# Two sums of the tail blocks moved from TensorE to GpSimd, and other durations in the clock that orders the work

## The chip, the cores and the metric

The kernel runs on one core of one Trainium2 chip. Its time is the device time of that core in microseconds (us). A core has five engines with a queue each: TensorE (PE, matrix products; its weight loads are shown as PEld), VectorE (DVE), ScalarE (ACT), GpSimd (POOL) and SyncE (SP, which here only issues DMA transfers). Each engine takes its queue strictly in order and waits at an instruction whose inputs are not there yet.

## The reference

Eight sequences of 512 rows and 128 features, float32, go through a stack with two kinds of block:

```python
x = x + 0.5 * moe(layernorm(x))            # 8 experts, 128 -> 512 -> 128, best 2 of 8 for each row
x = x + attention(layernorm(x))            # 16 heads of 8, causal, rotated q and k
x = x + 0.5 * moe(layernorm(x))            # the same weights again
x = x + 0.5 * fp6_linear(layernorm(x))     # rows rounded to 6-bit numbers in blocks of 32, times weight, + bias
x = x + scan_block(layernorm(x))           # gates g, v, d; h = a*h + sigmoid(g)*tanh(v); then a gated feed-forward
x = x + 0.5 * fp6_linear(layernorm(x))
```

In `scan_block`, with u its normed input, u becomes u + h, and the block gives u + W_out(silu(W_gate n) * (W_up n)) with n the RMS norm of u. Two sums matter below: 0.5 * bias in each `fp6_linear`, and the u that is added to what W_out gives.

## The kernel before, in words

A sequence is a tile `X[b]` of 128 partitions by 4 x 128 elements in SBUF; b runs from 0 to 7. X stays there all the time.

The first expert pass (stage 0) routes sequences 0 to 2, then 3 to 7; attention is stage 1; the second expert pass (stage 2) has the groups 0 to 4 and 5 to 7. After it come the *tails*: for each sequence `fp6`, `mix` (the scan block) and `fp6` again (`tail`, L1439). At most four tails are in flight (`flight`, L1447).

An expert pass works on row tiles of 256 rows that go to one expert. `moe_stream` (L676) routes a sequence: norm, scores (`lp`), two maxima, counts (`pt`), and then eight indirect DMAs on POOL that scatter its rows to a table in DRAM (`by_stretch`). `moe_tiles` (L846) then fetches, on SP, an expert's weights `wx` (578 KB) and 256 rows `xs` (L855 to L868), turns the rows (`xp`), and does the first product (`hp`, in two halves), the activation `hs` and the second product (`yp`); the sum `yo` goes back to DRAM on SP (`rows_out`, L922). The rows of a group are fetched only once all its sequences have been scattered (`sent`, L504). `moe_combine` (L960) gathers each row's two results on POOL (`y<-rows_out`) and adds them to X on DVE with their gates. The second group of stage 2 has 19 tiles, the first 27.

`fp6` (L1296): moments on DVE, a power on POOL (`rs`), the norm on ACT (`um`), the rounding on DVE (`am`, `sc`, `rs`, then five passes `q`), four transposes on PE (`tp_xd`), a copy on ACT (`uT_xd`), four products with the weight (`yp<-wd_t,uT_xd`) and the update of X on DVE (L1326). The bias comes into the same PSUM bank by a product of a row of ones with the bias (L1311). `mix` (L1332) goes on in the same way over all engines; its last step is the output product `yo` (L1425), into which u comes as a product with the identity (L1426), and the sum into X (L1437).

**What sets the order.** The kernel is written as generators (streams) that yield after a few instructions. All instructions of the tile streams go through the class `Clock` (L67): while the kernel is being built it estimates when each engine is free, and when a stream's next step is ready; `drive` (L146) lays side streams into attention, and `finish` (L164) always steps the stream that is ready first. So the durations that `took` (L82) returns decide the order in which instructions are put in the engines' queues, and nothing else: on the chip each engine waits for its inputs. Nearly all instructions are recorded by the helper in `_Logged`, so the profile gives them line L190; they are told apart by the names of their tiles.

Of the kernel before, what the change touches and what calls it, by code (L numbers as in the profile page):

```python
# [9 lines left out]
F32 = mybir.dt.float32  # L10
# [3 lines left out]
ALU = mybir.AluOpType  # L14
# [3 lines left out]
P = 128  # L18
S = 512
NT = S // P  # L20
# [5 lines left out]
NGF = 3  # L26
# [40 lines left out]
class Clock:  # L67
# [14 lines left out]
    def took(self, engine, op, out, args):  # L82
        shape = out.shape if out is not None else (1, 1)
        n = 1
        for k in shape[1:]:
            n *= k
        if engine == "tensor":
            strips = 4 if shape[0] == 32 or (len(args) > 1 and args[1].shape[0] == 32) else 1
            return 0.05 + 0.0016 * n / strips
        if engine == "vector":  # L90
            return 0.09 + 0.0011 * n
        if engine == "scalar":
            return 0.2 + 0.0008 * n
        if op == "indirect_dma_start":
            return 1.3
        if n <= 32:
            return 1.0
        return 0.2 + (0.0009 if op == "affine_select" else 0.0018) * n

    def account(self, ready, chained=True):  # L100

        end, last = ready, None
        product = ready
        for engine, op, out, args in self.log:
            took = self.took(engine, op, out, args)
            dep = end if chained and engine != last else ready
            if not chained and engine != "tensor":
                dep = product
            at = max(self.free[engine], dep) + took
            self.free[engine] = at  # L110
            if engine == "tensor":
                product = at
            end, last = (at if chained else max(end, at)) + 0.1, engine
            if op == "indirect_dma_start":
                end = at
            elif engine == "gpsimd":
                end += 0.5
        self.log.clear()
        return end
# [120 lines left out]
def kernel(  # L240
# [17 lines left out]
    nc = tc.nc  # L258
    ck = Clock(nc)
# [4 lines left out]
    cpool = ctx.enter_context(tc.tile_pool(name="const", bufs=1))  # L264
# [8 lines left out]
    X = []  # L273
# [24 lines left out]
    ident = cst[:, C_ID : C_ID + P]  # L298
# [51 lines left out]
    ):  # L350
        rest_of_consts[name] = (const_tile(f"{name}_s", ap, dtype), ap)
    rope_s, wattn_s, future_s, vec_s, wq8_s, wmix_s, wout_s = (t for t, _ in rest_of_consts.values())
    bq_s = cpool.tile([P, P], F32, tag="bq_s", name="bq_s")
    half_vec = cpool.tile([P, 2], F32, tag="half_vec", name="half_vec")

    clear_rows(1)
    for t, ap in rest_of_consts.values():
        nc.sync.dma_start(out=t, in_=ap)
    nc.sync.dma_start(out=bq_s, in_=bq.partition_broadcast(P))

    nstat, vpad = [], []
    for k in range(2):
# [3 lines left out]
    def clear_for_attention():  # L366

        for t in nstat:
            ck.gpsimd.memset(t, 0.0)
            yield  # L370


        for t in vpad:
            ck.gpsimd.memset(t, 0.0)
            yield
            ck.gpsimd.memset(by_pair(t)[:, :, :, DK : DK + 1], 1.0)
            yield
        ck.gpsimd.tensor_scalar_mul(half_vec[:, 0:1], vec_s[:, V_BG : V_BG + 1], 0.5)
        ck.gpsimd.tensor_scalar_mul(half_vec[:, 1:2], vec_s[:, V_BD : V_BD + 1], 0.5)
        yield  # L380
# [9 lines left out]
    def bank(name):  # L390
        return p_ps.tile([P, S], F32, tag="ps", name=name)
# [904 lines left out]
    def fp6(b, s):  # L1296

        name = f"{s}_{b}"
        mv = moments(X[b], name)
        rs = yield from power(mv[:, :, 1], 1e-5, name)  # L1300
        u = yield from normed_act(X[b], mv, rs, name, tag="um")

        xd = yield from quantized(
            u.rearrange("p t (g k) -> p (t g) k", k=FB), S // FB, name, rounding
        )
        yield from turning.take()
        tp = turned(xd.rearrange("p (t g) k -> p t (g k)", t=NT), f"xd_{name}")
        rounding.give()

        yp = bank(f"yp_{name}")  # L1310
        ck.tensor.matmul(  # L1311
            yp.rearrange("p (t d) -> p t d", t=NT), ones[0:1, :],
            bq_s[0:1].unsqueeze(1).to_broadcast([1, NT, P]), start=True, stop=False,
        )
        yield
        xt = wk.tile([P, S], F32, tag="uT", name=f"uT_xd_{name}")
        ck.scalar.copy(xt, tp)
        yield "product"
        for t in range(NT):
            ck.tensor.matmul(  # L1320
                yp[:, ts(t, P)], xt[:, ts(t, P)], wd_t, start=False, stop=(t == NT - 1)
            )
        turning.give()
        yield
        xb = X[b].rearrange("p t d -> p (t d)")
        ck.vector.scalar_tensor_tensor(xb, yp, 0.5, xb, ALU.mult, ALU.add)  # L1326
# [5 lines left out]
    def mix(b):  # L1332
# [81 lines left out]
        for f in range(NGF):  # L1414
# [6 lines left out]
            ck.vector.tensor_tensor(sg, sg, pu, ALU.mult)  # L1421
            sgs.append(sg)
            yield

        yo = bank(f"yo_{b}")  # L1425
        ck.tensor.matmul(yo, ident, uf, start=True, stop=False)  # L1426
        for t in range(NT):
            for f in range(NGF):
                ck.tensor.matmul(
                    yo[:, ts(t, P)], sgs[f][:, ts(t, P)], wout_s[:, f, :],  # L1430
                    start=False, stop=(t == NT - 1 and f == NGF - 1),
                )
        gating.give()
        feeding.give()
# [141 lines left out]
```

## Time and profile before

| | |
|---|---|
| time, median of 3 runs | 1116.26 us (1114.25 to 1118.13) |
| time of the profiled execution | 1195.04 us |
| its span, first to last instruction | 1193.3 us |
| mean granted TensorE clock in it | 0.920 |
| busy: PE, PEld | 995.5 us (83%), 693.5 us (58%) |
| busy: DVE, ACT, POOL | 683.6 us (57%), 494.9 us (41%), 472.8 us (40%) |
| moved by DMA | 127.34 MB, mean 107 GB/s |
| score products of attention, first and last | 264.0 us, 827.1 us |
| last store of an expert tile | 1042.1 us |
| last gather of expert results | 1098.2 us |

In a line of a profile a group of instructions is named by line, engine, operation and `out<-in`; `xN` counts them. Behind a bar stand busy time and the mean time of one in ns, and then the idle time of the engine before them with what ended it. In an engine's instructions in order of time, the first number is the start, the second the length, both in us, and a bracket gives the idle time before and what ended it ("issue" and "remote": nothing that the profile shows of this core's engines). A PE product of float32 is recorded as two instructions, and their times overlap.

### The profile page before, as it was taken

The page shows a single profiled execution, that of the slowest core. Times are in us where ns is not written, and L with a number is a line of the kernel's source. Part 1 is how long each engine was busy: PE and PEld are TensorE (multiplying, and loading weights), DVE is VectorE, ACT ScalarE, POOL GpSimd, SP SyncE. Part 2 cuts the span into 40 slices and gives each one's busy share as a digit, 9 for nine tenths or more (in the row PEclk, how much of TensorE's full clock was granted, in tenths as well). Part 3 has the DMA queues.
Part 4 walks back from the last instruction along what each step waited for, and adds up shares of the span by engine and source line. Part 5 has one row for each costly group of instructions (what it writes and reads, how often), then busy time and mean ns, then how long its engine had stood idle before and what let it go on. Part 6 is the DMA issues. An engine that isn't in the chain of part 4 may idle for free.

```text
span 1193.3 us, 20637 instructions
## 1 busy us (share of the span) xinstructions
PE 995.5 (83%) x6753; PEld 693.5 (58%) x6753; DVE 683.6 (57%) x2550; ACT 494.9 (41%) x1135; POOL 472.8 (40%) x627
## 2 busy tenths in 40 slices
PE   3351699799998998998998999999968898887795
PEld 2350598687774545555554567766957666554453
DVE  6040133355556888867676856532523775788755
ACT  1210233233354646464545444444312475544651
POOL 3647202331127658745363523214025452174210
PEclk9995799799999999989898889999979899995897
DMA  9542477487658001000000153334555550011000
GB/s 291 181 148 82 129 230 233 152 267 209 191 155 237 21 15 35 25 10 17 4 19 1 37 159 102 122 112 133 151 156 175 155 150 20 27 41 40 0 10 27
DMA packets 122363, 127.34 MB, mean 107 GB/s; under 512 B 9616, under 2 KB 103696, under 8 KB 122256
## 3 DMA queue, kind: packets, MB, share of 16 engines
q1 hardware_dynamic: 114064, 109.22, 30.4%
q0 software_dynamic: 8192, 16.79, 4.4%
q8 instruction: 54, 0.88, 0.3%
q14 instruction: 53, 0.43, 0.1%
HBM read 79.58 MB, written 46.40 MB: 106 GB/s over the span
## 4 chain that ended last, share of the span: by engine, by line
PE 57%; DVE 16%; issue 7%; another core or an unknown queue 7%; POOL 5%; ACT 4%; DMA 3%; SPq 1%; POOLq 0%; DVEq 0%; ACTq 0%
PE yp L190 13%; PE hp L190 11%; PE sa L190 9%; PE av L190 6%; PE sb L190 5%; DVE q L190 3%; POOL y L190 3%; DVE seen L190 2%; DVE x L190 2%; DVE st L190 1%; PE gt L190 1%; ACT um L190 1%; DMA y<-rows_out,at 1%; PE xp L190 1%
## 5 line engine op out<-in xcount | busy, mean ns | idle before, releaser
L190 DVE CUSTOM_DVE_ANT_0 seen<-sa,future_s 128x128 f32<-128x128 f32 (+3 forms) x512 | 225.2, 486 | 98.3 <-PE sb L190 70.5
L190 ACT ACTIVATE pm<-sb 128x512 f32<-128x512 f32 (+1 forms) x384 | 182.0, 525 | 205.0 <-PE sb L190 179.7
L190 PE MATMUL yp<-wx,hs 128*128 128x128 f32 x1472 | 207.3, 284 | 53.6 <-ACT hs L190 29.2
L190 ACT ACTIVATE hs<-hp,wx 128x256 f32<-128x256 f32 x276 | 119.8, 470 | 313.5 <-PE hp L190 188.4
L190 PEld LDWEIGHTS yp<-wx,hs 128*128 128x128 f32 x1472 | 193.1, 198 | 74.4 <-issue 34.5
L190 PE MATMUL sb<-qa,ka 32*128 32x512 f32 (+3 forms) x1024 | 222.7, 488 | 6.7 <-DVE nstat L190 4.8
L190 PE MATMUL sa<-ka,qz 32*128 32x384 f32 (+3 forms) x1024 | 211.3, 484 | 3.7 <-DVE nstat L190 2.5
L190 PE MATMUL hp<-xt,wx 128*128 128x256 f32 x736 | 204.5, 403 | 9.8 <-DVE g L190 5.3
L190 POOL TENSOR_SCALAR_AFFINE_SELECT pm<-pm 128x256 f32<-128x256 f32 x256 | 100.8, 409 | 240.3 <-ACT pm L190 229.3
L190 POOL DMA_INDIRECT y<-rows_out,at x128 | 134.9, 1054 | 137.7 <-DMA rows_out<-yo 77.9
L190 DVE TENSOR_SCALAR hs<-hp,wx 128x256 f32<-128x256 f32 x92 | 44.5, 483 | 214.6 <-ACT hs L190 196.6
L190 PEld LDWEIGHTS hp<-xt,wx 128*128 128x128 f32 x736 | 133.8, 201 | 39.7 <-issue 15.6
L190 PEld LDWEIGHTS sa<-ka,qz 32*128 32x128 f32 x1024 | 106.7, 194 | 71.8 <-issue 23.4
L190 PEld LDWEIGHTS sb<-qa,ka 32*128 32x128 f32 x1024 | 103.8, 190 | 30.5 <-DVE nstat L190 7.6
L190 POOL TENSOR_TENSOR rs<-rs,mhalf 128x4 f32<-128x4 f32 (+2 forms) x44 | 53.2, 1211 | 165.8 <-DVE rs L190 126.1
L190 PE MATMUL av<-pm,vpad 128*32 128x512 f32 (+3 forms) x1024 | 96.3, 472 | 2.8 <-POOL pm L190 2.6
L190 POOL DMA_INDIRECT by_stretch<-um,sat x64 | 64.3, 1005 | 30.6 <-DVE nt L190 13.4
L190 DVE SCALAR_TENSOR_TENSOR x<-y,g,x 128x128 f32<-128x128 f32 x128 | 47.5, 375 | 15.2 <-DMA y<-rows_out,at 11.0
L190 DVE TENSOR_TENSOR yo<-yp,wx 128x256 f32<-128x256 f32 x92 | 38.5, 418 | 29.8 <-PE yp L190 13.2
L190 POOL DMA_INDIRECT rows_in<-a,at x40 | 38.9, 971 | 28.2 <-issue 27.9
L190 PE MATMUL xp<-cst,xs 128*128 128x128 f32 x184 | 37.9, 293 | 11.5 <-DMA xs<-by_stretch 11.3
L190 ACT ACTIVATE um<-x,nb_um,rs 128x128 f32<-128x128 f32 x96 | 39.4, 484 | 17.2 <-DVE nb_um L190 11.3
(211 smaller groups left out, 1238.1 us busy)
## 6 DMA issues: line engine op xcount, KB each, us to landing
wx<-in_wexp SPq DMA_DIRECT2D x92, 578.0 KB
rows_out<-yo SPq DMA_DIRECT2D x92, 128.0 KB
by_stretch<-zero SPq DMA_DIRECT2D x8, 1280.0 KB
rows_in<-zero SPq DMA_DIRECT2D x2, 3456.0 KB
by_stretch<-zero SPq DMA_DIRECT2D x8, 768.0 KB
xs<-rows_in SPq DMA_DIRECT2D x46, 128.0 KB
xs<-by_stretch SPq DMA_DIRECT2D x46, 128.0 KB
x<-in_x SPq DMA_DIRECT2D x8, 256.0 KB
```

Source lines behind the costliest of these rows:

```text
L190: return call(*args, **kw)
```

## The change

Two sums leave TensorE. The bias, halved once on POOL (`half_bq`), is added to X on POOL, ahead of the products, and the product of ones with the bias goes; the four products with the weight now open the bank themselves. In `mix`, u is added to X on POOL before the output product, and the product with the identity goes. So 16 and 8 products leave, and 24 additions of 128x512 and one multiplication of 128x128 come to POOL.

`took` gives other durations for TensorE, VectorE and ScalarE, and `account` (L100) no longer lets a GpSimd `tensor_tensor` of over 1.1 us (which a 128x512 one is, by its estimate of 1.12) hold back the stream's next step. This applies to the new additions and to the two sums of the rotation in attention (`ta_q`, `ta_k`).

```diff
@@ took
         if engine == "tensor":
             strips = 4 if shape[0] == 32 or (len(args) > 1 and args[1].shape[0] == 32) else 1
-            return 0.05 + 0.0016 * n / strips
+            if op == "transpose":
+                return 0.15
+            return max(0.24, 0.02 + 0.00195 * n) if strips == 1 else 0.05 + 0.0016 * n / strips
         if engine == "vector":
-            return 0.09 + 0.0011 * n
+            return 0.17 + 0.001 * n
         if engine == "scalar":
-            return 0.2 + 0.0008 * n
+            return 0.28 + 0.00068 * n
@@ account
             self.free[engine] = at
+            if engine == "gpsimd" and op == "tensor_tensor" and took > 1.1:
+                continue
             if engine == "tensor":
                 product = at
@@ constants
-    bq_s = cpool.tile([P, P], F32, tag="bq_s", name="bq_s")
+    half_bq = cpool.tile([P, P], F32, tag="half_bq", name="half_bq")
...
-    nc.sync.dma_start(out=bq_s, in_=bq.partition_broadcast(P))
+    nc.sync.dma_start(out=half_bq, in_=bq.partition_broadcast(P))
@@ clear_for_attention
+        ck.gpsimd.tensor_scalar_mul(half_bq, half_bq, 0.5)
         ck.gpsimd.tensor_scalar_mul(half_vec[:, 0:1], vec_s[:, V_BG : V_BG + 1], 0.5)
@@ fp6
-        yp = bank(f"yp_{name}")
-        ck.tensor.matmul(
-            yp.rearrange("p (t d) -> p t d", t=NT), ones[0:1, :],
-            bq_s[0:1].unsqueeze(1).to_broadcast([1, NT, P]), start=True, stop=False,
+        ck.gpsimd.tensor_tensor(
+            X[b], X[b], half_bq.unsqueeze(1).to_broadcast([P, NT, P]), ALU.add
         )
         yield
         xt = wk.tile([P, S], F32, tag="uT", name=f"uT_xd_{name}")
         ck.scalar.copy(xt, tp)
         yield "product"
+        yp = bank(f"yp_{name}")
         for t in range(NT):
-            ck.tensor.matmul(
-                yp[:, ts(t, P)], xt[:, ts(t, P)], wd_t, start=False, stop=(t == NT - 1)
-            )
+            ck.tensor.matmul(yp[:, ts(t, P)], xt[:, ts(t, P)], wd_t, start=True, stop=True)
@@ mix
-
+        ck.gpsimd.tensor_tensor(X[b], X[b], u, ALU.add)
         yo = bank(f"yo_{b}")
-        ck.tensor.matmul(yo, ident, uf, start=True, stop=False)
         for t in range(NT):
             for f in range(NGF):
                 ck.tensor.matmul(
                     yo[:, ts(t, P)], sgs[f][:, ts(t, P)], wout_s[:, f, :],
-                    start=False, stop=(t == NT - 1 and f == NGF - 1),
+                    start=(f == 0), stop=(f == NGF - 1),
                 )
```

## The prediction

> **What bounds the kernel now.** First I read the page's busy times, then stretches of the span by engine, then each engine in order of time where the stretches show idle TensorE.
>
> ```profile
> PE 995.5 (83%) x6753; PEld 693.5 (58%) x6753; DVE 683.6 (57%) x2550; ACT 494.9 (41%) x1135; POOL 472.8 (40%) x627
> 867.00:892.00 25.00, 13.70 (x76) 11.41 (x75) 6.41 (x22) 2.61 (x7) 4.86 (x5) 0.76 0.46 144
> 892.00:1041.00 149.00, 131.03 (x704) 100.40 (x703) 91.91 (x286) 76.87 (x197) 59.98 (x55) 0.94 0.37 111
> 1041.00:1193.30 152.30, 115.06 (x460) 68.79 (x458) 108.19 (x306) 69.05 (x173) 47.00 (x41) 0.83 0.08 24
> ```
>
> TensorE is the bound over all (83%). The three stretches (columns: length, busy PE, weight loads, DVE, ACT, POOL, clock, DMA) are where the change works: a hole of 25 us, the last 19 expert tiles mixed with the first tails, and tails alone. In the last PE is busy 76% and DVE 71%: neither is a bound by itself; the in-order queues are.
>
> The hole, on PE, then on SP's queue, then on ACT:
>
> ```profile
> 877.24 4.16 PE L190 MATMUL yp<-wx,hs 128*128 128x128 f32 x24
> 885.49 0.66 PE L190 MATMUL xp<-cst,xs 128*128 128x128 f32 x2 [4.08 <-DMA xs<-by_stretch]
> 888.55 0.69 PE L190 MATMUL xp<-cst,xs 128*128 128x128 f32 x2 [2.40 <-DMA xs<-by_stretch]
> 891.63 0.69 PE L190 MATMUL xp<-cst,xs 128*128 128x128 f32 x2 [2.39 <-DMA xs<-by_stretch]
> ```
> ```profile
> 860.73 19.27 SPq L922 DMA_DIRECT2D rows_out<-yo  x5
> 880.87 0.35 SPq L857 DMA_DIRECT2D wx<-in_wexp  x1
> 882.63 0.39 SPq L868 DMA_DIRECT2D xs<-by_stretch  x1
> ```
> ```profile
> 871.84 0.84 ACT L190 ACTIVATE hs<-hp,wx 128x256 f32<-128x256 f32 x2 [4.75 <-issue]
> 874.68 1.20 ACT L190 ACTIVATE hs<-hp,wx 128x256 f32<-128x256 f32 x3 [2.00 <-remote]
> ```
>
> The second expert pass has 27 tiles for its first group and 19 for its second; the second group's may be fetched only after the last sequence (7) is routed and scattered. Its scatters end at 873.2, but SP stands behind five stores of the first group's last tiles until 880, because the fetches were written into its queue after them. PE has nothing left and waits for xs three times. Tiles run 3.75 us apart before this (first halves start at 859.96, 863.69, 867.43). The first half of tile 26 starts at 870.94, so the next tile was due at 874.7; it comes at 892.1: 17.4 us lost, of which ACT's two pauses (6.75 us) are not SP's doing.
>
> **The change part by part.**
>
> *The build clock* gives other durations, so the queues are written in another order though no work differs. I compared the two built orders.
>
> (a) Up to the middle of attention nearly nothing moves (first PE difference: row 422 of 2138). Routing of the second pass stands 26 to 50 score matmuls later, and the first expert tile of that pass 44 later; at the end of attention 2.8 fewer tiles are done. Those 2.8 tiles are then left as cover: before, 4.5 tiles follow the routing's count matmul (pt, 857.4); after, 7, or 26 us. SP's queue now has the fetches of the second group's first two tiles ahead of the stores of tiles 23 and 24. Counting from pt: scatters end at +15.8 (row 873.2 minus 857.4), land about +18, the first xs is fetched at +18.5 and lands at +21.5 (882.63 to 885.49 is 2.9), the second some 2.3 later; PE arrives at +26. The hole's SP part, 10.6 us (17.4-6.75), closes; if ACT's pauses were a result of the drained queue, 17.4. What waits behind SP's earlier wait: the store of tile 23, ready at about +18 and issued at about +21; two yo buffers let tile 25 start at +26, so nobody is late. I take -12, ends -5 and -17.
>
> (b) Fewer tiles inside attention make it less well filled. Without tiles a sequence takes 57.9 us (y at 572.46 and 630.35) for 128 score matmuls, 0.452 each. From 697.9 to 829, 172 of them, 16.5 tiles (62 us) and 6 us of projections take 131: 0.366 each. 44 x 0.086 = +3.8; I take +3.5.
>
> *Sums off TensorE.*
>
> ```profile
> L190 PE MATMUL yp<-bq_s,ones 1*128 1x512 f32 x32 | 23.5, 821 | 0.0
> L190 PE MATMUL yo<-um_m,cst 128*128 128x512 f32 x16 | 8.8, 637 | 0.0
> L190 POOL TENSOR_TENSOR ta_k<-ta_k,tb_k 128x512 f32<-128x512 f32 x8 | 10.2, 1281 | 12.9 <-DVE tb_k L190 12.9
> ```
>
> (c) 16 bias products and 8 identity products go (two records each). Their busy times overlap neighbours; on the chain a warm yp of 10 records takes 2.14 and of 8 1.07 to 1.09, so a bias is 1.07, and an identity product 0.86. 16 x 1.07 + 8 x 0.86 = 24 us off a queue that is busy 76 to 88% here. Between transposes and yp the bias fills the time in which ACT copies (0.58), so alone it hides 0.6 of its 1.07. One case stands bare: in the last chain yp took 4.02 for 10 at the low clock, 2.07 of it bias, with the copy over 0.75 after its start: -1.25 there. From both sides: 0 (DVE and latency decide) to -24. Near the chain of waits of the last stretch, where yp is 11.5% and yo 6.9% of 152 us, half of yp and a quarter of yo are these products: 8.7+2.6=11. Another wait takes over for some: I take -8.
>
> (d) 24 adds of 128x512 come to POOL: 24 x 1.27 = 30.5 us (the rows of the same form, 1261 to 1281 ns). POOL is busy 107 of 301 us here, and its queue also holds the gathers y (1.0+0.3 us each) and the powers rs (1.0 to 1.7), which every norm waits for. An add has its inputs long before, so it blocks by its length, not by a wait; its readers wait little, as xT copy and yp (1.7) cover 1.27. One halving of the bias joins POOL at about 128 us, where POOL is idle to 198.6 and the bias has been in flight since 36.6: nothing. The price is elsewhere:
>
> ```profile
> 368.95 1.30 POOL L190 TENSOR_TENSOR ta_q<-ta_q,tb_q 128x512 f32<-128x512 f32 x1 [0.33 <-DVE tb_q L190]
> 368.79 1.62 DVE L190 SCALAR_TENSOR_TENSOR x<-y,g,x 128x128 f32<-128x128 f32 x2
> 374.60 0.73 DVE L190 SCALAR_TENSOR_TENSOR x<-y,g,x 128x128 f32<-128x128 f32 x2
> ```
>
> Two weighted sums, both inputs in SBUF, take 1.62 beside such an add and 0.73 alone: DVE stood 0.89 us and went on when POOL was done. Operations with one input in PSUM (yo, 0.42 at 253.84 under an add) did not. The Trainium skill, page "SBUF — State Buffer", section "SBUF: two separate sides", says the same more strongly: a DVE operation with two SBUF inputs and a GpSimd one that reads SBUF hold a shared port pair exclusively, and the loser waits out the whole instruction. By the rule at its worst, all 24 adds stop DVE for 1.27: +30.5, and the change is slower. By the row, 24 x 0.89 = 21.4 if each meets such an operation. In the tails these are four q passes (2.76 us per rounding, 16 times), gtg and scan (1.92, 8 times) and 64 weighted sums (22): 81 of 301 us. A quarter of the adds meets one running and then stops the next of a q chain (0.9 of 1.27); of the rest some 40% lose 0.6: 0.42 each, 10 us of DVE, which is on the chain most of the time. I take +7, ends 0 and +30.
>
> (e) *Order of the tails.* In the new PE order tiles stand ahead of tails: at the last tile's second product about 1.5 tails' work is done, before 2.6. Those 1.1 tails (15 us of PE) no longer delay the last tile, so the gathers of sequences 5 to 7, the last at 1098.17 now, can come up to 15 sooner beyond (a). Against it, tails lose the cover of tiles, and the end is written in series: sequence 6's output product yo stands behind sequence 5's last rounding, 7's behind 6's. Now the three yo start 9 to 10 us apart (1149.60, 1158.72, 1169.03); in series each needs x, a rounding up to yp and yo, about 17: +14.6 if the sequences arrive as close as now. Since they arrive staggered, I take -5, ends -25 and +14.6.
>
> Sum: -12+3.5-8+7-5 = -14.5, so 1195.0 to 1180.5 for the profiled execution. The median, 1116.3, is 78.8 below it; part of the profile's pauses is probably its own, so I carry the difference, not the ratio: 1101.8, say 1102.
>
> **The rivals.**
>
> R1, the forecast above: 1102; its own range 1092 to 1112. Chance 0.45.
>
> R2, more than forecast: the hole closes whole (-17) and sequence 7 starts as much sooner as its data allow (-20), the rest as above: 1116.3-17+3.5-8+7-20 = 1082. For: b7's moments start at 1101.98, right after its last gather. Against: flight slots (four) free only as tails end. 0.17.
>
> R3, slower: the port. If an add costs DVE its whole length, 24 x 1.27 = 30.5 in place of 7: 1125. It decides from 0.9 us an add (21.5/24), just what the row shows for one that meets. For: a rounding is a run of such operations. Against: DVE idles 29% in the last stretch. 0.20.
>
> R4, the serial end costs its full +14.6: 1121. For: PE takes its queue in order. 0.10.
>
> R5, the change doesn't do what it says: PE's relief and the closed hole turn into waits elsewhere, 1113 to 1119, centre 1116. 0.08.
>
> **How the numbers follow.** Within 0.3% of 1116.3 (1112.9 to 1119.6, about what a measurement here can tell from none) counts as same. Faster: all of R2, nearly all of R1 (0.42 of 0.45) and a little of R5: 0.60. Same: the rest of R1, most of R5: 0.10. Slower: R3, R4: 0.30. The range leaves out the far ends of R2 and R3: 1079 to 1128.
>
> **What would show it.** (a) PE waits for xs under 3 us in all between tile 26 and the second group's first tile; SP's fetches ahead of the stores. (b) attention ends about 7 us sooner with 2.8 fewer tiles done. (c) yp x8 in place of x10 on the chain. (d) roundings' q passes or weighted sums above 1.0 us beside POOL adds of 1.27; DVE busy up by about 10. (e) last gather before 1085; yo of 5, 6, 7 over 12 us apart means R4. Wrong if the fetches wait for routing that now comes later, or q passes lengthen by 20 us or more in sum.

## The result, and the profile after

The changed kernel takes 1106.73 us (median of 6 runs, 1105.19 to 1111.97) where the kernel before, on the same chip, takes 1113.48 (1110.49 to 1118.13). The ratio is 0.9943, with a 95% interval of 0.9915 to 0.9971: 0.6% faster, 6.4 us by the ratio. 1102 was forecast, with a range of 1079 to 1128. So the direction and the range hold; of the forecast gain of 14.5 us less than half was measured.

The first profile of the kernel before has a span of 1193.3 us, and attention begins in it at 264.0. In a second one (experiment 1) the span is 1112.0 us and attention begins at 198.9: of the 81 us of pauses 65 lay ahead of attention. All differences below are taken against the second profile, where nothing else is said. In the page of the changed kernel the first line of busy times reads:

```profile
PE 963.0 (87%) x6705; PEld 682.8 (62%) x6705; DVE 705.7 (64%) x2550; ACT 495.8 (45%) x1135; POOL 506.7 (46%) x652
```

and in that of the kernel before, profiled again:

```profile
PE 973.0 (88%) x6753; PEld 676.8 (61%) x6753; DVE 684.0 (62%) x2550; ACT 495.5 (45%) x1135; POOL 475.7 (43%) x627
```

TensorE has 48 records less. DVE has not one instruction more, and is busy 21.7 us longer. POOL has 25 instructions more.

The stretches of the span show where the time went. The cuts are the first and the last score product of attention, the last count product of the second pass's routing (pt), the end of the last expert tile, and the end. Columns: length, busy PE, weight loads, DVE, ACT, POOL, granted clock, DMA share, GB/s. First the kernel before (second profile):

```profile
198.90:759.40 560.50, 525.53 (x4267) 328.66 (x4267) 376.64 (x1557) 270.70 (x586) 252.04 (x409) 0.96 0.29 85
759.40:789.80 30.40, 29.71 (x222) 25.32 (x220) 12.19 (x45) 11.71 (x27) 3.41 (x4) 1.00 0.57 173
789.80:958.70 168.90, 147.00 (x847) 115.93 (x847) 104.87 (x337) 83.09 (x211) 69.24 (x63) 0.95 0.41 126
958.70:1112.00 153.30, 114.53 (x455) 67.39 (x453) 107.85 (x304) 69.08 (x173) 47.16 (x41) 0.83 0.08 24
```

and the changed kernel:

```profile
197.70:739.70 542.00, 516.46 (x4181) 319.24 (x4181) 372.06 (x1546) 266.24 (x577) 249.57 (x407) 0.97 0.28 83
739.70:772.20 32.50, 32.29 (x236) 26.83 (x234) 12.23 (x45) 12.25 (x29) 5.16 (x6) 1.00 0.57 169
772.20:898.10 125.90, 119.54 (x780) 104.59 (x780) 82.47 (x263) 61.07 (x151) 62.73 (x57) 0.99 0.61 184
898.10:1110.30 212.20, 137.90 (x544) 92.05 (x543) 155.36 (x388) 95.36 (x242) 85.27 (x72) 0.78 0.06 20
```

Attention is 18.5 us shorter, and the stretch with the last tiles 43.0: the last tile ends 60.6 us sooner. Of that nearly all is gone at the end: from the last tile on it takes 58.9 us longer, with TensorE busy 65% where it was 75%. Part of this is only work put off (tails that ran beside tiles now run after them), part is loss. The experiments tell part of this apart. The granted clock of the last stretch is lower, too: 0.78 where it was 0.83.

**The hole is closed.** SP's queue of the kernel before, second profile (start, length, what is issued; the fetch of the weights between these lines is left out here and below):

```profile
792.74 14.74 SPq L922 DMA_DIRECT2D rows_out<-yo  x5
810.09 0.39 SPq L868 DMA_DIRECT2D xs<-by_stretch  x1
```

and of the changed kernel:

```profile
786.00 4.00 SPq L927 DMA_DIRECT2D rows_out<-yo  x2
792.31 0.39 SPq L873 DMA_DIRECT2D xs<-by_stretch  x1
```

The five stores ahead of the fetches have become two, and the first rows of the second group are fetched at 792.31, where TensorE still has tile 26 to do. TensorE's queue in the kernel before, second profile (the two halves of tile 26, then the first tile of the second group):

```profile
802.95 1.03 PE L190 MATMUL hp<-xt,wx 128*128 128x256 f32 x4
804.70 1.03 PE L190 MATMUL hp<-xt,wx 128*128 128x256 f32 x4
813.16 0.66 PE L190 MATMUL xp<-cst,xs 128*128 128x128 f32 x2 [4.75 <-DMA xs<-by_stretch]
819.14 4.31 PE L190 MATMUL hp<-xt,wx 128*128 128x256 f32 x12
```

and of the changed kernel, where no product waits:

```profile
795.45 1.03 PE L194 MATMUL hp<-xt,wx 128*128 128x256 f32 x4
797.21 1.03 PE L194 MATMUL hp<-xt,wx 128*128 128x256 f32 x4
799.66 1.13 PE L194 MATMUL hp<-xt,wx 128*128 128x256 f32 x4
```

In the kernel before the first halves of these two tiles start 16.2 us apart, now 4.2, where 3.7 is usual. So 12.0 us came back. The second profile has no pauses of ACT of the kind that the first one showed here: ACT waits for TensorE (14.90 us before 821.14).

**Attention lost a wait that the forecast didn't price.** TensorE's waits within attention, kernel before (total us, times, longest):

```profile
PE pt L190 <- DVE k L190: 9.5, 4, 2.7
```

and changed kernel:

```profile
PE pt L194 <- DVE k L194: 1.3, 1, 1.3
```

The count product of the routing stood so early in TensorE's queue that it waited for DVE four times. Written 26 to 50 score products later, it waits once. By the table of stretches TensorE's idle time within attention falls by 9.4 us (from 35.0 to 25.5); these waits are 8.2 of it, and what other waits lost and gained there comes to little in sum.

**DVE stands beside the additions.** DVE's queue of the changed kernel in the tails (start, length; lines between these left out):

```profile
951.27 1.63 DVE L194 TENSOR_TENSOR q<-q,q 128x512 f32<-128x512 f32 x1
952.94 1.63 DVE L194 TENSOR_TENSOR q<-q,sc 128x512 f32<-128x512 f32 x1
957.89 2.30 DVE L194 TENSOR_SCALAR q<-q 128x512 int32<-128x512 int32 x2
1059.36 0.68 DVE L194 TENSOR_REDUCE am<-um 128x16 f32<-128x512 f32 x1
```

and POOL's queue at the same times:

```profile
951.02 1.34 POOL L194 TENSOR_TENSOR x<-x,half_bq 128x512 f32<-128x512 f32 x1
952.32 1.71 POOL L194 TENSOR_TENSOR x<-x,um_m 128x512 f32<-128x512 f32 x1
958.16 1.27 POOL L194 TENSOR_TENSOR x<-x,half_bq 128x512 f32<-128x512 f32 x1
1059.08 1.27 POOL L194 TENSOR_TENSOR x<-x,half_bq 128x512 f32<-128x512 f32 x1 [6.19 <-ACT um L194]
```

Two passes of the rounding take 1.63 us each in place of 0.69: each ends 0.55 us after an addition has ended. Two one-input passes take 2.30 together in place of 0.89. Not every operation stands: the reduction `am` at 1059.36 keeps its 0.68 us although an addition runs all the while (from 1059.08), and so does the update of u at 1058.76 (one input in PSUM), which the same addition overlaps by half.

**The end is more in series.** TensorE's queue of the changed kernel over its last sequences (lines between these left out):

```profile
1034.80 1.16 PE L194 MATMUL yp<-wd_t,uT_xd 128*128 128x128 f32 x8
1039.23 0.61 PE L194 MATMUL yo<-wout_s,silu 128*128 128x128 f32 x4
1045.44 4.16 PE L194 MATMUL yo<-wout_s,silu 128*128 128x128 f32 x20 [5.60 <-DVE silu L194]
1068.28 3.40 PE L194 MATMUL yo<-wout_s,silu 128*128 128x128 f32 x24
1085.48 2.07 PE L194 MATMUL yp<-wd_t,uT_xd 128*128 128x128 f32 x8 [0.67 <-ACT uT_xd L194]
1087.35 4.07 PE L194 MATMUL yo<-wout_s,silu 128*128 128x128 f32 x24
1102.18 1.11 PE L194 MATMUL tp_xd<-cst,q 128*128 128x128 f32 x4 [10.76 <-DVE q L194]
```

and in the kernel before, second profile:

```profile
1068.22 2.84 PE L190 MATMUL yo<-wout_s,silu 128*128 128x128 f32 x24
1077.34 2.84 PE L190 MATMUL yo<-wout_s,silu 128*128 128x128 f32 x24
1087.66 2.84 PE L190 MATMUL yo<-wout_s,silu 128*128 128x128 f32 x24
```

The last three output products of the changed kernel start at 1039.23 (most of the first one only at 1045.44), 1068.28 and 1087.35, so 29 and 19 us apart, in the kernel before 9 and 10. That is the form which the rival R4 described. The same products also take longer here: `yp` 2.07 us where it took 1.16 at 1034.80, `yo` 4.07 where it takes 2.84 in the kernel before. From 1080 on the granted clock is 0.66, in the kernel before 0.79. How much of the end is the form and how much the clock was not separated.

### The profile page after: what moved, and what is told of

It reads as the page before. It is cut to its first block, busy times and chain, and to the rows that moved or that the text cites. A ratio compares the mean times of both kernels' runs of the same rounds, so it can differ in the third digit from the quotient of the medians.

```text
span 1110.3 us, 20582 instructions
## 1 busy us (share of the span) xinstructions
PE 963.0 (87%) x6705; PEld 682.8 (62%) x6705; DVE 705.7 (64%) x2550; ACT 495.8 (45%) x1135; POOL 506.7 (46%) x652
## 4 chain that ended last, share of the span: by engine, by line
PE 65%; DVE 16%; ACT 6%; issue 5%; DMA 4%; POOL 3%; SPq 1%; POOLq 0%; DVEq 0%; ACTq 0%
PE yp L194 13%; PE hp L194 12%; PE sa L194 10%; PE av L194 7%; PE sb L194 6%; DVE q L194 4%; DVE x L194 3%; PE yo L194 3%; PE lp L194 2%; POOL y L194 2%; DVE seen L194 1%; PE xp L194 1%; ACT um L194 1%; DVE st L194 1%; DMA rows_out<-yo 1%
## 5 line engine op out<-in xcount | busy, mean ns | idle before, releaser
L194 PE MATMUL sb<-qa,ka 32*128 32x512 f32 (+3 forms) x1024 | 225.6, 476 | 10.6 <-DVE nstat L194 8.5
L194 PE MATMUL sa<-ka,qz 32*128 32x512 f32 (+3 forms) x1024 | 208.1, 472 | 3.1 <-DVE nstat L194 2.9
L194 PE MATMUL yp<-wx,hs 128*128 128x128 f32 x1472 | 197.8, 277 | 3.3 <-DVE hs L194 3.3
L194 PEld LDWEIGHTS yp<-wx,hs 128*128 128x128 f32 x1472 | 185.5, 192 | 19.8 <-issue 10.5
L194 PE MATMUL hp<-xt,wx 128*128 128x256 f32 x736 | 195.2, 389 | 0.1
L194 PEld LDWEIGHTS hp<-xt,wx 128*128 128x128 f32 x736 | 128.9, 195 | 19.4 <-issue 4.2
L194 PEld LDWEIGHTS sb<-qa,ka 32*128 32x128 f32 x1024 | 106.9, 187 | 38.7 <-DVE nstat L194 13.1
L194 PE MATMUL av<-pm,vpad 128*32 128x512 f32 (+3 forms) x1024 | 93.1, 459 | 1.1 <-POOL pm L194 0.9
L194 POOL DMA_INDIRECT by_stretch<-um,sat x64 | 64.2, 1003 | 29.3 <-DVE nt L194 13.8
L194 DVE SCALAR_TENSOR_TENSOR x<-y,g,x 128x128 f32<-128x128 f32 x128 | 52.6, 414 | 17.7 <-DMA y<-rows_out,at 15.6
L194 DVE COPY xt<-xp 128x256 f32<-128x256 f32 x92 | 38.2, 416 | 12.3 <-PE xp L194 12.3
L194 PEld LDWEIGHTS av<-pm,vpad 128*32 128x32 f32 x1024 | 23.6, 109 | 35.7 <-issue 20.5
```

Of the source, the lines that this page charges most:

```text
L194: return call(*args, **kw)
```

## The experiments

Theory T1 was: the new order gains, and the additions give most of it back by making VectorE stand, through the port that GpSimd and VectorE share. Rival T2: the additions cost by holding up POOL's own queue. Rival T3: the order of the tails is what decides, and the sums matter little. Ratios are against the kernel before on the same chip, with 95% intervals; 1% is 11.1 us. The kernel before was measured again on each chip, with medians of 1113.1 to 1115.9 us.

**1. The kernel before again.** No edit.

> The kernel before, unchanged, for a second profile: the first one holds pauses of some 80 us in the first expert pass that the profile of the changed kernel lacks, so the two can't be compared in whole. Expected by all theories: a span of 1110 to 1117 us, attention starting near 198 us in place of 264.0, DVE busy 684 us, and the hole between the two groups of the second expert pass still there, TensorE waiting for xs two to four times within 20 us after tile 26. If the hole is gone in an execution without pauses, step (a) of the prediction rested on a disturbance.

Span 1112.0 us, attention from 198.9, and the hole as shown above. So step (a) did not rest on a disturbance.

**2 and 3. Each part of the change alone.** In 2 the sums stay on TensorE; in 3 the durations and the rule are as before. Against the changed kernel, in part:

```diff
@@ experiment 2, fp6 and mix: as before the change, with `took` and `account` as after
-        ck.gpsimd.tensor_tensor(
-            X[b], X[b], half_bq.unsqueeze(1).to_broadcast([P, NT, P]), ALU.add
-        )
+        yp = bank(f"yp_{name}")
+        ck.tensor.matmul(
+            yp.rearrange("p (t d) -> p t d", t=NT), ones[0:1, :],
+            bq_s[0:1].unsqueeze(1).to_broadcast([1, NT, P]), start=True, stop=False,
+        )
...
@@ experiment 3, took and account: as before the change, with the sums as after
-            return 0.17 + 0.001 * n
+            return 0.09 + 0.0011 * n
...
-            if engine == "gpsimd" and op == "tensor_tensor" and took > 1.1:
-                continue
```

> The new durations and the rule on long GpSimd additions alone; both sums stay on TensorE. By my theory (the closed hole gains, the port on the two sums loses): 12 to 17 us from the hole, less 3.5 in attention, and the end in series costs some: -8 to -14 us against before, so 1100 to 1106, at least as fast as the changed kernel; DVE busy at 684, not 706. If the gain is TensorE's relief by the 24 products: -2 to +3 here. If the order of the tails, with tails in series at the end, is what eats the gain: also 0 to -4 here.

> Both sums on GpSimd, the old durations; the hole between the groups stays, and the end of the tails is less in series than in the changed kernel. By my theory: relief of 8 us against 15 to 20 us of DVE standing at the port, so +5 to +12 us, 1119 to 1126, DVE busy up by 15 to 22 us. If the additions cost nothing on the path, as the idle DVE of the last stretch would allow: -8 us, 1106. If the serial end is the main loss of the changed kernel: -3 to 0.

Measured: the clock alone 1.0020 (0.9995 to 1.0045), 1116.83 us; the sums alone 1.0221 (1.0183 to 1.0259), 1139.34 us. No theory expected both, and the second loses more than any expected: each part alone gains nothing or loses, and together they gain. In 2 attention is about as short as in the changed kernel (544.7 us, 542.0 there) and the hole is closed, and yet the end comes no sooner. But here two things change at once: with other instructions the clock also writes other tails. The sums and the order had to be separated.

**4 to 7. Two orders, three places for the sums.** The clock can be told of instructions that are not issued, and instructions can be issued without telling it. So the order of every queue was held fixed, once as in the changed kernel, once as in the kernel before, and only the sums were exchanged. (In the profiles of all kernels of one order VectorE, ScalarE, GpSimd and SyncE carry out their other instructions in the same sequence.) Experiments 4 and 7 leave out the bias and u, so their results lack these two sums. For the additions left out of the changed kernel:

```diff
@@ fp6
-        ck.gpsimd.tensor_tensor(
-            X[b], X[b], half_bq.unsqueeze(1).to_broadcast([P, NT, P]), ALU.add
-        )
+        ck.log.append(("gpsimd", "tensor_tensor", X[b], ()))
@@ mix
-        ck.gpsimd.tensor_tensor(X[b], X[b], u, ALU.add)
+        ck.log.append(("gpsimd", "tensor_tensor", X[b], ()))
```

and for the products in its order, in part (the other two are the same with the kernel before's log entries):

```diff
@@ fp6, from the changed kernel
+        ck.log.append(("gpsimd", "tensor_tensor", X[b], ()))
+        yp = bank(f"yp_{name}")
+        nc.tensor.matmul(
+            yp.rearrange("p (t d) -> p t d", t=NT), ones[0:1, :],
+            half_bq[0:1].unsqueeze(1).to_broadcast([1, NT, P]), start=True, stop=False,
         )
...
@@ mix
+        ck.log.append(("gpsimd", "tensor_tensor", X[b], ()))
         yo = bank(f"yo_{b}")
+        nc.tensor.matmul(yo, ident, u.rearrange("p t d -> p (t d)"), start=True, stop=False)
```

> The changed kernel in the same order on every queue, with the 24 additions of 128x512 on GpSimd left out, so the half bias and u are missing from the result: the price of the additions alone. By my theory DVE's busy time falls by about 22 us, back to 684, and of that 10 to 18 us come off the end: 1089 to 1097. If DVE's stops lie in its idle time: within 3 us of the changed kernel, 1104 to 1107, with DVE still down by 22. If the additions cost by holding up GpSimd's queue (gathers and powers), the gain is above DVE's 22 us, 1080 to 1085.

> The order of the changed kernel on every queue, but with the sums back on TensorE (the 24 products are put in where the old kernel has them, the 24 additions are not issued). Together with the run without additions it gives the price of the products in this order. By the prediction's step (c), 8 us: 1094. If TensorE's relief is worth all of the 24 us of its busy time: 1110. If the products cost more than that, because each stands between an arriving input and the products that everything waits for: above 1112. If it is below 1100, the changed kernel's order is good and the additions alone spoil it; if it is at 1110 or above, the order gains nothing with the sums on TensorE, and the loss is in the tails.

> The order of the kernel before on every queue, with the 24 additions on GpSimd in the place of the 24 products: the sums moved, the order not touched. By the port theory the additions cost 20 us here as in the other order and the products give back what they cost: 1108 to 1125. If the old order's tiles and tails mix so well that the relief of TensorE counts in full while DVE has room: 1100. The run with the old durations and the sums moved, whose order differs, was at 1139; if this one is there too, the sums and not the order cost those 24 us.

> The order of the kernel before, with neither the products nor the additions, so the bias and u are missing from the result. Against the kernel before it gives the price of the products in the old order, against the run with additions the price of these. By step (c) of the prediction: -8, 1106. If TensorE's relief counts in full: -24, 1090. If the changed order's end in series costs nothing, this run lies 12 us or more above the run without additions in the new order (1086), by the closed hole and the tighter attention; if the new order's tails eat that, both are within 5 us.

Measured medians: 1085.85, 1103.83, 1125.03 and 1104.61 us. Experiment 4 gained more than T1 expected and a little less than T2's range; 5 lies between the 1094 of step (c) and the 1110 of TensorE's full relief; 6 is at the upper end of what T1 expected; 7 is near step (c).

| ratio to the kernel before | products on TensorE | additions on POOL | neither |
|---|---|---|---|
| order of the kernel before | 1 | 1.0104 (1.0068 to 1.0141) | 0.9912 (0.9879 to 0.9946) |
| order of the changed kernel | 0.9898 (0.9870 to 0.9926) | 0.9943 (0.9915 to 0.9971) | 0.9743 (0.9704 to 0.9782) |

Read along the rows: the additions cost 1.92% or 21.4 us in the old order and 2.00% or 22.3 us in the new one. The products cost 0.88% or 9.8 us in the old order and 1.55% or 17.3 us in the new one. Moving the sums therefore loses in both orders: 11.6 us in the old, 5.0 in the new, where the two intervals only just overlap. Read down the columns: the order alone gains 11.4 us with the products, 18.0 with the additions and 18.8 with neither. Each of these differences is good to some 3 to 6 us. The whole gain of the change is the order's. T3 is right in that, and wrong in that the sums don't matter. Moving the sums loses 11.6 us where the old order is kept, and 24.6 in experiment 3, where the old durations write another order for them: 13 us of that loss are order too. One thing goes with the sums in the new order: with the products, `yp` takes its PSUM bank ahead of ScalarE's copy, without them behind it, while in the old order it takes it ahead throughout. What this makes of the 17.3, the 18.0 and the 18.8 was not separated; the 11.4 is free of it.

Without the additions, and with nothing else altered, DVE is busy 22.3 us less, by the page of that kernel:

```profile
PE 958.3 (88%) x6705; PEld 680.8 (63%) x6705; DVE 683.4 (63%) x2550; ACT 496.4 (46%) x1135; POOL 473.6 (44%) x628
```

The time falls by as much, 22.3 us, to some 5 us. In the old order the additions make DVE busy 17.7 us longer (701.6 us in experiment 6, 683.9 in 7), and the price there is 21.4 us. So about what DVE stood came off the end in both.

**8. POOL's queue held by fills.** Each addition is replaced by two fills of a tile that nobody waits for; the bias and u are left out:

```diff
-        ck.gpsimd.tensor_tensor(X[b], X[b], u, ALU.add)
+        for _ in range(2):
+            nc.gpsimd.memset(nstat[0], 0.0)
+        ck.log.append(("gpsimd", "tensor_tensor", X[b], ()))
```

> The changed kernel with each addition replaced by two fills of a tile that nobody waits for (128x512 each, 0.55 us, no input in SBUF), so GpSimd's queue is held as long as before and the bias and u are missing from the result. If the additions cost by the port that they share with DVE's two-input operations: DVE busy back to 684 and the time near the run without additions, 1085 to 1091. If they cost by holding up gathers and powers in GpSimd's queue: near the changed kernel, 1101 to 1107. If fills stop DVE as well: DVE busy stays above 695.

Measured 0.9779 (0.9728 to 0.9830), 1086.56 us. The page of this kernel:

```profile
PE 953.8 (88%) x6705; PEld 675.7 (62%) x6705; DVE 685.0 (63%) x2550; ACT 495.8 (46%) x1135; POOL 498.7 (46%) x676
```

POOL is busy 25.1 us more than without additions, 1.05 us for each (an addition took 1.37), DVE only 1.6 us more, and the time is 4.0 us higher, with intervals that overlap. So of the additions' 22.3 us some 18, give or take 6, go with what additions do and fills don't, and at most a few with POOL's queue being held. T2 falls as the main cause. Fills differ from additions in two more ways, on which the trace of the changed kernel bears: no instruction in it waits for an addition's result, and DVE's waits for POOL's powers (`rs`) are the same with and without additions (6.9 and 7.0 us), for the gathers 6.7 and 3.0. But three additions waited for `um` themselves, 10.2 us in all with POOL's queue behind them, where the prediction had their inputs ready long before; what this cost was not separated. The groups show where DVE stood. Changed kernel (busy us, mean ns of one, then idle before):

```profile
L194 DVE TENSOR_TENSOR q<-q,q 128x512 f32<-128x512 f32 x16 | 15.2, 949 | 0.6
L194 DVE TENSOR_SCALAR q<-q 128x512 int32<-128x512 int32 x16 | 11.9, 741 | 0.6
L194 DVE TENSOR_SCALAR sc<-am 128x16 f32<-128x16 f32 x16 | 6.2, 384 | 0.6
L194 DVE SCALAR_TENSOR_TENSOR x<-yp,x 128x512 f32<-128x512 f32 x16 | 11.0, 688 | 13.7 <-PE yp L194 13.7
```

and with the fills:

```profile
L194 DVE TENSOR_TENSOR q<-q,q 128x512 f32<-128x512 f32 x16 | 11.1, 692 | 0.6
L194 DVE TENSOR_SCALAR q<-q 128x512 int32<-128x512 int32 x16 | 7.3, 459 | 0.5
L194 DVE TENSOR_SCALAR sc<-am 128x16 f32<-128x16 f32 x16 | 3.6, 228 | 0.6
L194 DVE SCALAR_TENSOR_TENSOR x<-yp,x 128x512 f32<-128x512 f32 x16 | 11.0, 687 | 13.3 <-PE yp L194 12.9
```

The first three lines change, the one-input passes among them (the second and third). Of the 22.2 us between the changed kernel and experiment 4, group by group, 7.7 are in these two. The last line, the update from PSUM, shows nothing either way here, as no addition of this execution ran beside one.

The fills are not without effect on DVE. Its queue and POOL's in experiment 8:

```profile
999.66 0.60 DVE L194 TENSOR_SCALAR sc<-am 128x16 f32<-128x16 f32 x1
1000.59 0.69 DVE L194 TENSOR_TENSOR q<-um,rs 128x512 f32<-128x512 f32 x1
1019.72 1.60 DVE L194 TENSOR_SCALAR q<-q 128x512 int32<-128x512 int32 x2
999.13 1.10 POOL L1316 MEMSET nstat<- 128x512 f32 x2
1000.29 1.11 POOL L1427 MEMSET nstat<- 128x512 f32 x2
1019.77 1.27 POOL L1316 MEMSET nstat<- 128x512 f32 x2
```

The one-input passes that meet a fill stand (`sc` 0.60 us in place of 0.175, two passes 1.60 together in place of 0.89), a pass with two inputs in SBUF keeps its 0.69. So passes of both kinds stand beside additions, and only the one-input ones beside fills; few of those met a fill.

**9. The bias product made cheap.** If moving the sums loses, the products can be made shorter where they are. The order is the changed kernel's, both sums are on TensorE; the bias is cut once, early, into three bfloat16 parts on three ranges of partitions, and one bfloat16 product sums them. Against experiment 5, in part:

```diff
@@ clear_for_attention
+        for lo, hi in ((0, 64), (64, 96), (96, P)):
+            nc.gpsimd.memset(part_s[lo:hi], 1.0 / (hi - lo))
+            nc.vector.tensor_copy(bq_parts[lo:P], half_bq[lo:P])
+            if hi < P:
+                nc.vector.tensor_tensor(half_bq[lo:P], half_bq[lo:P], bq_parts[lo:P], ALU.subtract)
@@ fp6
-            yp.rearrange("p (t d) -> p t d", t=NT), ones[0:1, :],
-            half_bq[0:1].unsqueeze(1).to_broadcast([1, NT, P]), start=True, stop=False,
+            yp.rearrange("p (t d) -> p t d", t=NT), part_s,
+            bq_parts.unsqueeze(1).to_broadcast([P, NT, P]), start=True, stop=False,
```

> The order of the changed kernel with both sums on TensorE, and the bias product made cheap: the bias is cut once into three bfloat16 parts that lie on different partitions, and one bfloat16 product sums them, in place of the float32 product of a row of ones (two records of 0.8 us). Nothing is left out. If the products' price in this order (1.73% of the time, 19 us, from the runs with and without them) follows their TensorE time, of which the 16 bias products are some 17 of 24 us, two thirds of it come back: 1090 to 1094. If that price is the wait for the bank or the two additional instructions, and not their length: 1101 to 1104.

Measured 0.9822 (0.9772 to 0.9873), 1094.03 us. Its bias product in the groups:

```profile
L1324 PE MATMUL yp<-bq_parts,part_s 128*128 128x512 bf16 x16 | 6.8, 427 | 0.0
```

and that of experiment 5, the same order with the float32 product:

```profile
L1317 PE MATMUL yp<-half_bq,ones 1*128 1x512 f32 x32 | 21.7, 764 | 0.0
```

14.9 us of TensorE less in this product, and 8.5 us less at the end (0.9898 to 0.9822, with intervals that just overlap). That is about half of the products' price, where two thirds were expected. TensorE as a whole is busy 23.0 us less (983.3 to 960.3), at a granted clock of 0.959 where it was 0.948; the clock's part was not separated. This version is faster than both kernels, with nothing left out.

**10. Old durations for the tails alone.** Sums on TensorE, new durations and rule, but a step of a tail is counted with the old durations:

```diff
+        if self.old:
...
+            if engine == "vector":
+                return 0.09 + 0.0011 * n
...
+        self.old = gen in self.tails
         self.slack[gen] = 0.0 if hint == "product" else 0.7
```

> Both sums on TensorE; the new durations order everything but the steps of the tails, which are counted with the old ones. Up to the last score product the order is that of the changed kernel; the tails come in another order, with their last output products not in series. The run with the new durations throughout was at 1.002 of before, the one with the changed kernel's order at 0.990, for the same instructions. If the new order of the tails is what gives back the 20 us gained in attention and at the hole: 1090 to 1096. If tails without tiles beside them cost that whatever their order: 1102 to 1110.

Measured 1.0007 (0.9984 to 1.0031), 1115.67 us. This kernel, experiment 2 and experiment 5 have the same instructions and the same order until the tails, and attention takes 544.2, 544.7 and 541.8 us in them. Yet they stand at 1.0007, 1.0020 and 0.9898. So the order of the tails alone moves this kernel by 12 us, but not because the old durations' tails are good: those measured the same as the kernel before. That is neither of the two expectations. Nor is it the series at the end: the last three output products are 28.7 and 7.0 us apart in experiment 10 and 12.8 and 26.0 in 2, against 30.7 and 20.3 in the faster 5. What these two have in common is that the last expert tile ends later (at 919.3 and 911.2, against 896.7 in 5); whether that is what costs them 12 us was not tested.

**11. The durations without the rule.** One execution of the changed kernel without the rule, additions on POOL:

```diff
-            if engine == "gpsimd" and op == "tensor_tensor" and took > 1.1:
-                continue
```

> The changed kernel without the rule on long GpSimd additions, so only the durations differ from the old clock; one look, for the length of attention. In the kernel before, the stretch of attention without expert tiles (score products 256 to 1664 in their order) takes 316 us, in the changed kernel 305. If the durations alone do that: 305 here. If the rule does it, by letting the stream that rotates q and k go on while GpSimd still adds: 316.

1095.97 us in one execution; attention 533.1 us, its stretch without tiles 297.3. That is below both expectations. So the durations alone shorten attention, and the rule is not needed for it. Seven profiles of kernels with the rule put this stretch between 304.7 and 309.2, so 297.3 could be a gain or a good execution.

**12. Both of the last two together.** The durations without the rule, sums on TensorE, bias in parts:

> The durations without the rule on long GpSimd additions, in the order that they give when the additions are counted, with both sums on TensorE and the bias product in bfloat16 parts. Nothing is left out. The run without the rule was 11 us below the changed kernel in one execution, 9 of them in attention; sums with the bias in parts were 13 us below the additions in the changed kernel's order. If the two add up: 1080 to 1085. If the single execution was a good one and attention gains nothing when measured again: 1091 to 1095, as the bias in parts alone.

Measured 0.9804 (0.9735 to 0.9874), 1089.68 us, attention 540.2 and its stretch 303.5. That is not to be told from experiment 9, and just under the range expected if the gains don't add up. The 297.3 did not come again. It is, with experiment 9, the fastest version that computes everything: 2% under the kernel before, 1.4% under the changed one.

## Why the prediction was right, and where its steps were not

1102 against 1106.73 measured, and the direction right. But 14.5 us of gain were forecast and 6.4 came, and the steps were less right than their sum: (b) and (c) gained more than forecast, (d) and (e) lost more, and that these nearly cancelled was luck.

**(a) The hole: -12 forecast, -12.0 shown.** TensorE's waits for xs are gone, by the mechanism named: two stores ahead of the fetches, not five. The split of the hole was not right. The prediction set 6.75 us of ACT's pauses apart and left 10.6 for SP; in the execution without such pauses the hole was 12.4, with 8.9 of waiting for xs in it, and 12.0 of it went.

**(b) Attention: +3.5 forecast, about -7 shown. This step had the wrong sign.** Attention took 18.5 us less. At its end 32.5 tiles of the pass are left where 29.4 were, near the 2.8 fewer of the prediction, and 3.1 tiles at 3.73 us are 11.7 us that are only put off; 6.8 is gain. The step asked only what fewer tiles leave unfilled. That routing comes 26 to 50 products later stood in the text as a fact about order, with no price. Its price was in the first profile too: pt waited for k for 9.4 us, four times, in a queue where everything stands behind it. 8.2 us of it went, against the 6.8 gained in all; the 1.4 between them has the sign of the step's own loss by fewer tiles, but other waits changed too. No experiment moved the count products alone.

**(c) 24 products off: -8 forecast, -9.8 in the old order and -17.3 in the new.** The estimate from the chain of waits was the value for the order that it was read from. That products stand in the way more where tails run without tiles would explain the rest, but it was not shown: the two values differ by hardly more than their intervals, and in the new order the place of the bank changed with the products. Even there it isn't the 24 us of TensorE's busy time.

**(d) The additions: +7 forecast, +22.3 shown. This term of the sum was mis-sized.** R3 had the price: 0.92 us of DVE for each addition (22.1 of busy time over 24, against the first profile; 0.74 in the old order), which is R3's own deciding point. The shares (a quarter of the additions stops one operation in full, 40% of the rest lose 0.6) were a guess at how often an addition meets something, and they came to 0.42 (0.41 by the shares as given) where 0.92 was shown. That an operation with one input in PSUM goes on held where one met an addition (u at 1058.76 in the changed kernel, 0.68 us; the update `x<-yp` at 972.04 in experiment 11, 0.68 within an addition of 1.73). But the list of those that stop was too short: one-input passes stop as well (q int32 435 to 741 ns, sc 201 to 384 against the kernel before), while others don't (`am` 680 to 681, the reciprocal 253 in both). The five q passes together lengthened by 15.9 us, short of the 20 that the prediction named as a sign of being wrong. The Trainium skill says this on the page that the prediction cites, "SBUF — State Buffer", in the section "SBUF: two separate sides": it names operations in a 2-port mode beside those with two SBUF inputs, and the prediction used only the second half. The trace agrees in that passes of both kinds stood beside additions (741 and 949 ns in place of 435 and 692), and that only one kind stood beside fills; that the one-input passes run in such a mode no run here shows. And DVE was put down as on the chain most of the time, which fits: 22.3 us of standing, 22.3 us at the end, 17.7 and 21.4 in the old order.

**(e) Order of the tails: -5 forecast, a loss of some 5 to 11 us shown. Wrong sign.** Its size is what is left over, in profiles of equal instructions (experiments 1 and 5): from the last pt to the end 322.2 against 330.7 us, +8.5, although the hole is 12.0 shorter and only 2.5 tiles, 9.3 us, more are left: 8.5+12.0-9.3 = +11.2. With neither sum, experiments 7 and 4: 1.6+12.5-9.3 = +4.8. The step took the last gather, which is what tails wait for first, as what the end follows. The last gather did come sooner (998.4 against 1017.0 in the second profile, by 18.6), but from it to the end it takes 112 us where it took 95, with TensorE busy for less of the time and at a lower clock. R4's serial end came, but that it is the cause was not shown, and the experiments speak against it: the last three output products are 26 and 19 us apart in experiment 9, which is among the fastest, and 29 and 7 in 10, which gains nothing. What in the order of the tails costs the time stays open.

The sum again with what was shown: -12.0-6.8-17.3+22.3 = -13.8, and -6.4 measured leaves +7.4 for (e), within the 4.8 to 11.2 above. R1's total came near because (b) and (c) gained some 20 us more than forecast and (d) and (e) lost some 28 more.

Of the signs named beforehand: xs waits under 3 us, yes; attention sooner by 7 us, no, by 18.5, with 3.1 tiles fewer, near the 2.8; yp x8, yes; DVE busy up by 10, no, by 22; last gather before 1085, yes, but that bound came from the disturbed profile and told nothing; the output products over 12 us apart, yes, which was to mean R4, but went with fast and slow orders alike.

## What to carry to other kernels

Price moved instructions by the waits that they cause where they stand now: a product that waits early in an in-order queue can be a gain as soon as anything writes it later, and the table of waits of the old profile shows its size. An elementwise operation moved to GpSimd beside a stream of short VectorE operations is to be charged as VectorE's time, with a good half to two thirds of its own length (0.74 of 1.27 us in the old order, 0.92 of 1.37 in the new), and, if VectorE's results are what the end waits for, as the end's. Shortening the product where it is (three bfloat16 parts) was worth more than moving it. When a change alters both the work and what orders the work, hold one order fixed and exchange only the work: each half alone, with its own order, had told two wrong stories here.

## What was not expected of the hardware

One-input passes of 128x512 on VectorE, 427 to 435 ns alone, and even a 128x16 one of 175, wait out a GpSimd addition (up to 3.09 us for one such pass, two additions in a row), while a reduction of the same 128x512 does not (676 ns within an addition). The waiting goes both ways: additions that take 1.27 us alone took 1.62 to 1.71 six times in the changed kernel, each beside VectorE passes that stood; in the old order (experiment 6) none took over 1.29. Fills by GpSimd of the same 128x512, 0.53 us each, left the passes with two inputs in SBUF alone (0.69 us beside them), but a one-input pass that met one stood (0.60 in place of 0.175); few met one, so VectorE's busy time hardly shows it (685.0 us against 683.4 without them). And for a kernel this dense, the order of the same instructions on the same queues was worth 12 us, more than the change as a whole.
